# Row copies by SP in place of one gather in 48, in a two-layer graph network

## The chip, the cores and the metric

The kernel runs on one core of a Trainium2 chip. The metric is the device time of one execution in microseconds, the median of a few runs. The engines are named as in the profile: PE (matrix multiplications; PEld loads its weights), DVE (vector engine), ACT (scalar engine), POOL (GpSimd) and SP (SyncE, which here only issues DMAs). Data lies in HBM, in SBUF (128 partitions) and in PSUM, where PE writes its results.

## The reference

Two layers of message passing on 6250 nodes with 128 features and 200,000 edges that are sorted by destination. `_layernorm` and a relu come before each layer, and each layer's output is added to x.

```
# layer 0: attention over a node's incoming edges, 8 heads of 16
z  = (feat @ W).reshape(N, 8, 16);  el, er = <z, attn_l>, <z, attn_r>
e  = leaky_relu(el[src] + er[dst], 0.2)
a  = exp(e - segment_max(e, dst)[dst])
out = segment_sum(z[src] * a, dst) / max(segment_sum(a, dst), 1e-9) + bias

# layer 1: an equivariant message layer
s, v = s @ W_up_s, v @ W_up_v             # per node, before the edges
w0..w3 = silu(silu(edge_feats @ A1 + b1) @ A2 + b2) @ A3      # per edge
mji = [ss*y_s*w0, (vs.y_v)/R3*w3, ss*y_v*w1, vs*y_s*w2]       # ss, vs = s[src], v[src]
out = (segment_sum(mji, dst) / 10) @ W_out
```

What matters here: in both layers every edge needs the row of its source node, `z[src]` with `el[src]` (136 floats) in the first layer and `[s, v][src]` (128 floats) in the second.

## The kernel before

The 200,000 edges are cut into 1563 tiles of 128, one edge to a partition, and the tiles into 98 blocks (NB) of 16 (KB); the last block has 11. A block covers a window of 128 nodes, of which 64 are shared with the next block; a segment sum is a matrix product of a one-hot tile (`one_hot`, L1043) with the tile's messages, summed in one PSUM bank over a block.

**The start** (to about 60 us) normalizes x, multiplies it with W and writes the table `t0` to HBM (`to_table`, L791 to L797, by SP). The source indices of all edges lie in SBUF as `src_col` (partition = edge of the tile, column = tile). A check that the edges are spread evenly is made on the device; its outcome is one word, which every engine loads into a register (`values_load`, L957). After that branch `even_edges` runs.

**Gathers.** `gather` (L832) issues for each tile one indirect DMA on POOL's queue: 128 rows of the table at the indices in one column of `src_col`, into one of the 16 places of a block's buffer `g` (name `z` in the code). There are five such buffers.

**First layer.** One pass of the loop handles three blocks at different stages: `take_rows(g + 3)` issues the gathers three blocks ahead, `logits` (L1112) adds the gathered `el` to `er` for the whole block, `maxima`, `neighbours` and `weights` form the softmax, `weighted` (L1166) scales the rows, `sums` (L1171) does the products. Every second block finishes 128 nodes. `node_x` to `node_s` then normalize them and multiply by W_up, and write a tile of the second table `t1` (`node_s`, L1224 and L1226, by SP, from the tile `sv`, of which there are two). `with_bias` (L1177) loads a tile of x by SP and adds the bias.

**Second layer.** The loop takes units of four tiles, four units to a block. `take_rows(b + 2)` gathers two blocks ahead; `network(b + 1)` computes the edge network one block ahead from two tiles that SP loads (`ft` and `yb`, L1410 and L1412, three buffers each); `messages` (L1458 to L1467, DVE) and `sums1` (L1475) follow. `node1` multiplies finished nodes by W_out, adds x and has SP write the output (L1489, L1491).

**The order of the work.** On PE, DVE and ACT the instructions stand in the order of the program:

```
in_order = {mybir.EngineType.PE, mybir.EngineType.DVE, mybir.EngineType.Activation}
with tc.manual_schedule(engines=in_order), ...
```

On SP and POOL a scheduler orders them. It put all 49 loads of x in one run at the start of the first layer; the writes of `t1` follow as `sv` comes. An engine handles its instructions one after the other, and one that waits for a semaphore holds those behind it. Each DMA of SP counts up one of eight semaphores in turn; a DMA waits, on its semaphore, for the one eight places before it.

Of the kernel before, what the change touches and what calls it, by code (L numbers as in the profile page):

```python
# [9 lines left out]
F32 = mybir.dt.float32  # L10
BF = mybir.dt.bfloat16
I32 = mybir.dt.int32
# [6 lines left out]
P = 128  # L19
# [3 lines left out]
ZW = F + H  # L23
# [940 lines left out]
def even_edges(tc, v):  # L964
# [7 lines left out]
    with ExitStack() as ctx:  # L972
# [3 lines left out]
        def gathered(table, tiles, width):  # L976
            return gather(z_pool.tile([P, KB, ZW], F32, name="g"), table, tiles, width)
# [59 lines left out]

        s_pool = ctx.enter_context(tc.tile_pool(name="fs", bufs=16))

        def one_hot(t, m, iota=iota):  # L1040

            s = s_pool.tile([P, 4, P], F32, name="s")
            nc.vector.tensor_tensor(s[:, :m], iota[:, None, :].to_broadcast([P, m, P]),  # L1043
                                    dloc[:, t : t + m].unsqueeze(2).to_broadcast([P, m, P]),
                                    OP.is_equal)
            return s
# [12 lines left out]
            return carry, agg  # L1059


        in_order = {mybir.EngineType.PE, mybir.EngineType.DVE, mybir.EngineType.Activation}
        with tc.manual_schedule(engines=in_order), \
                tc.tile_pool(name="l0", bufs=2) as l0, \
                tc.tile_pool(name="l0n", bufs=2) as l0n, \
# [106 lines left out]
                                     start=c["o"] + k == 0, stop=c["o"] + k == KT[c["b"]] - 1)  # L1172


            def with_bias(i, n):
                x_i = x_all[:, i : i + n, :]
                nc.sync.dma_start(x_i, xp[i * P : (i + n) * P].rearrange("(j p) f -> p j f", p=P))  # L1177
                nc.vector.tensor_add(x_i, x_i, bias_b[:, None, :].to_broadcast([P, n, F]))

            def node_x(u):  # L1180
# [35 lines left out]
            def node_s(u):  # L1216
                i, n, p_n = u["i"], u["n"], u["p_n"]
                for j in range(n):
                    nc.tensor.matmul(p_n[:, 2 + j, :], u["h_t"][:, j, :], wup, start=True, stop=True)
                sv = l0n.tile([P, 2, P], F32, name="sv")  # L1220
                nc.scalar.activation(sv[:, :n], p_n[:, 2 : 2 + n], AF.Copy, scale=PRE)
                first = i * P - W0
                if i == 0:
                    nc.sync.dma_start(t1[: P - W0, :], sv[W0:, 0, :])  # L1224
                else:
                    nc.sync.dma_start(t1[first : first + n * P].rearrange("(j p) f -> p j f", p=P),  # L1226
                                      sv[:, :n])
# [13 lines left out]
            def take_rows(g):  # L1241
                if 0 < g < NG:
                    c = cs[g]
                    t = c["b"] * KB + c["o"]
                    c["z"] = gathered(t0, range(t, t + c["kt"]), ZW)

            def bank_of(c, bank="p_u"):
                if c["o"] == 0:
# [36 lines left out]
            nc.vector.memset(st["ends"], 0.0)  # L1285
            none = {"kt": 0, "b": 0, "o": 0}
            c5, c4, c3, c2, c1 = cs[NG - 5 :]
            for g in range(NG - 3):
                take_rows(g + 3)
                c, b4 = cs[g], (cs[g - 1] if g else None)  # L1290
                n1 = cs[g + 1] if g + 1 < NG else none
                n2 = cs[g + 2] if g + 2 < NG else none
                nodes = []
                logits(c)
                ends_of(n2, 0)
                if n1 is not none:
                    masks_of(n1)
                turned(n1, 0)
                maxima(c)
                ends_of(n2, 1)  # L1300
# [24 lines left out]
                if b4:  # L1325
                    sums(b4, 0)
                for n in nodes:
                    node_t(n)
                if n1 is not none:
                    er_sum(n1)  # L1330
                ends_of(n2, 3)
                for n in nodes:
                    node_s(n)
                if b4:
                    sums(b4, 8)
                if g == NG - 4:
                    for q in range(4):
                        ends_of(c1, q)
                    masks_of(c1)
                    for q in range(4):  # L1340
                        turned(c1, q)
                        er_of(c1, q)
                    er_sum(c1)
            with_bias(NX - 2, 2)

            logits(c3)
# [43 lines left out]
            node_t(u)  # L1390
            node_x(w)
            node_s(u)
            for step in (node_d, node_h, node_t, node_s):
                step(w)


        with tc.manual_schedule(engines=in_order), \
                tc.tile_pool(name="l1", bufs=3) as l1, \
                tc.tile_pool(name="l1n", bufs=2) as l1n, \
                tc.tile_pool(name="l1_ps", bufs=2, space=PSUM) as l1_ps:  # L1400

            def network(b, step):

                c = blk[b]
                q0, second = step // 2 * 4, step % 2
                if 2 * q0 >= KT[b]:
                    return
                if step == 0:
                    c["ft"] = l1.tile([P, P], F32, name="ft")
                    nc.sync.dma_start(c["ft"], f8[:, b, :])  # L1410
                    c["yb"] = l1.tile([P, KB, 4], F32, name="yb")
                    nc.sync.dma_start(c["yb"], y4[:, b * KB : (b + 1) * KB, :])  # L1412
                    c["h2"] = []
                if step == 3 or 2 * q0 + 8 >= KT[b] and second:
                    c["yp"] = held[:, P + b % 3 * KB * 3 : P + (b % 3 + 1) * KB * 3].rearrange(
                        "p (t i) -> p t i", i=3)
                    nc.scalar.copy(c["yp"], c["yb"][:, :, 1:4])  # L1417
                p_h = l1_ps.tile([P, 4, P], F32, name="p_h")
                if not second:
                    for q in range(4):  # L1420
                        nc.tensor.matmul(p_h[:, q, :], a1p[:, q0 + q, :], c["ft"], start=True, stop=True)  # L1421
                    c["h1"] = l1.tile([P, 4, P], F32, name="h1")
                    nc.scalar.activation(c["h1"], p_h, AF.Silu, bias=b1)  # L1423
                else:
# [53 lines left out]
            def node1(i, agg):  # L1478
                x_i = x_all[:, i, :]
                p_n = l1_ps.tile([P, 4, P], F32, name="p_n", bufs=1)  # L1480
                for q in range(2):
                    nc.tensor.transpose(p_n[:, q, :], agg[:, q * P : (q + 1) * P], ident)
                m_t = l1n.tile([P, 2, P], F32, name="m_t")
                nc.scalar.copy(m_t, p_n[:, :2])
                for q in range(2):
                    nc.tensor.matmul(p_n[:, 2, :], m_t[:, q, :], wout[:, q, :], start=q == 0, stop=q == 1)
                nc.vector.scalar_tensor_tensor(x_i, p_n[:, 2, :], POST, x_i, op0=OP.mult, op1=OP.add)
                if i == 0:
                    nc.sync.dma_start(out[: P - W0, :], x_all[W0:, 0, :])  # L1489
                else:  # L1490
                    nc.sync.dma_start(out[i * P - W0 : (i + 1) * P - W0, :], x_i)  # L1491
# [11 lines left out]

            def take_rows(b):
                if b < NB:
                    blk[b]["z"] = gathered(t1, range(b * KB, b * KB + KT[b]), P)

            for b in range(2):
                take_rows(b)
            for step in range(4):  # L1510
                network(0, step)
# [5 lines left out]
            for i, u in enumerate(us):  # L1517
                b, k0, m = u["b"], u["k0"], u["m"]
                if k0 == 0:
                    take_rows(b + 2)  # L1520
                if b + 1 < NB:
                    network(b + 1, k0 // 4)
                if i + 1 < NU:
# [5 lines left out]
                if ends is not None:  # L1529
# [1 line left out]
                    if ends % 2 == 1:  # L1531
                        done.append((ends // 2, agg))
                    ends = None
                for a in ready:
                    node1(*a)
                ready, done = done, []
                sums1(u)
                if k0 + m == KT[b]:
                    ends = b
            for a in ready:  # L1540
                node1(*a)

            p_u = blk[NB - 1]["p_u"]
            nc.vector.tensor_copy(both[:WB, 0, :], agg[:WB, :])
# [156 lines left out]
```

## Time and profile before

| | us |
|---|---|
| median of 3 runs | 4023.37 (4021.22 to 4023.41) |
| the profiled execution | 4015.26 |
| its span in the profile | 4013.5 |
| first layer, from about 60 to | 2046 |
| second layer, gathers from 2046.9 to | 3997 |
| PE, DVE, ACT, POOL busy | 2837.4, 2191.8, 1374.3, 2993.5 |

| what SP does | count | hold of SP, median ns |
|---|---|---|
| loads of x tiles (L1177) | 49 | 430 |
| writes of `t1` (L1226) | 48 | 320 |
| edge loads (L1410, L1412) | 98 + 98 | 328, 328 |
| outputs (L1491) | 47 | 344 |

A group in the profile names the line, engine and operation, output and input tiles, the count, then busy time in us with the mean of one in ns, then the idle time of the engine ahead of these instructions and what ended most of it. "issue" is idle time in which the engine waited for nothing that the profile shows. Waits name the waiting instruction, what it waited for, the total in us, how often, and the longest. A window's row gives its start and end, its length, busy time with count of PE, PEld, DVE, ACT and POOL, the granted clock of PE, the share of the DMA engines' time in use, and GB/s. Rows of one line give the shortest, median and longest duration of an instruction in ns. SPq, ACTq and so on stand for instructions that the engine's sequencer handles itself: DMA issues, semaphore waits, register loads.

### The profile page before, as it was taken

The page shows a single profiled execution, that of the slowest core. Times are in us where ns is not written, and L with a number is a line of the kernel's source. Part 1 is how long each engine was busy: PE and PEld are TensorE (multiplying, and loading weights), DVE is VectorE, ACT ScalarE, POOL GpSimd, SP SyncE. Part 2 cuts the span into 40 slices and gives each one's busy share as a digit, 9 for nine tenths or more (in the row PEclk, how much of TensorE's full clock was granted, in tenths as well). Part 3 has the DMA queues.
Part 4 walks back from the last instruction along what each step waited for, and adds up shares of the span by engine and source line. Part 5 has one row for each costly group of instructions (what it writes and reads, how often), then busy time and mean ns, then how long its engine had stood idle before and what let it go on. Part 6 is the DMA issues. An engine that isn't in the chain of part 4 may idle for free. (4 is left out here: it accounts for less than half of the span.)

```text
span 4013.5 us, 45637 instructions
## 1 busy us (share of the span) xinstructions
PE 2837.4 (71%) x14592; PEld 2369.6 (59%) x14592; DVE 2191.8 (55%) x5376; ACT 1374.3 (34%) x3450; POOL 2993.5 (75%) x3158
## 2 busy tenths in 40 slices
PE   3666666666666666666677777777787777787787
PEld 3665655565556555555665665565666555666565
DVE  4544444444444444444456666666666666666666
ACT  3322222222222222222333434344434343443443
POOL 6777777777777777777757777777777777777776
PEclk6666666666666666666679999999999999999999
DMA  7222222222222222222212222222222222222221
GB/s 206 57 57 58 57 58 57 58 57 58 57 58 57 58 58 58 57 58 57 58 48 60 60 59 61 59 60 59 60 60 60 59 61 59 60 59 60 60 60 51
DMA packets 174105, 248.25 MB, mean 62 GB/s; under 512 B 70944, under 2 KB 123072, under 8 KB 173856
## 3 DMA queue, kind: packets, MB, share of 16 engines
q0 software_dynamic: 100032, 211.47, 19.7%
q1 hardware_dynamic: 73536, 33.70, 3.1%
q8 instruction: 118, 1.93, 0.2%
q14 instruction: 131, 1.07, 0.1%
q10 hardware_dynamic: 288, 0.07, 0.0%
HBM read 234.73 MB, written 9.99 MB: 61 GB/s over the span
## 5 line engine op out<-in xcount | busy, mean ns | idle before, releaser
L832 POOL DMA_INDIRECT g<-ft,fsrc x3110 | 2959.7, 952 | 975.4 <-issue 892.3
L1475 PE MATMUL p_u<-mj,s 128*128 128x256 f32 x3126 | 802.8, 401 | 354.7 <-DVE mj L1467 354.0
L1475 PEld LDWEIGHTS p_u<-mj,s 128*128 128x128 f32 x3126 | 582.8, 195 | 547.3 <-DVE mj L1467 478.2
L1171 PE MATMUL p_u<-g,s 128*128 128x136 f32 x3062 | 581.8, 369 | 0.5 <-DVE g L1166 0.5
L1171 PEld LDWEIGHTS p_u<-g,s 128*128 128x128 f32 x3062 | 557.2, 273 | 0.6 <-DVE g L1166 0.6
L1458 DVE TENSOR_TENSOR vy<-g,p_i 128x384 f32<-128x384 f32 x391 | 216.5, 554 | 596.3 <-DMA g<-ft,fsrc 569.3
L1442 ACT ACTIVATE p_w<-p_w,yb 128x64 f32<-128x64 f32 x1563 | 450.3, 288 | 113.6 <-PE p_w L1438 73.5
L1112 DVE TENSOR_TENSOR e_s<-g,er 128x128 f32<-128x128 f32 (+1 forms) x98 | 28.4, 290 | 749.3 <-DMA g<-ft,fsrc 749.2
L1438 PE MATMUL p_w<-fa3p,h 128*128 128x256 f32 x1564 | 403.8, 381 | 0.0
L1088 PE MATMUL p_d<-fident,s 128*128 128x128 f32 x1563 | 392.8, 418 | 5.1 <-DVE s L1043 5.1
L1116 PE MATMUL pe<-fident,e_s 128*128 128x128 f32 x98 | 39.7, 406 | 454.0 <-DVE e_s L1113 454.0
L1438 PEld LDWEIGHTS p_w<-fa3p,h 128*128 128x128 f32 x1564 | 285.7, 193 | 120.9 <-issue 57.4
L1081 ACT COPY mk<-p_m 128x385 f32<-128x385 f32 (+1 forms) x99 | 47.6, 481 | 903.1 <-PE p_m L1078 903.1
L1088 PEld LDWEIGHTS p_d<-fident,s 128*128 128x128 f32 x1563 | 318.9, 229 | 43.6 <-DVE s L1043 31.6
L1423 ACT ACTIVATE h<-p_h,fb 128x512 f32<-128x512 f32 x196 | 134.7, 687 | 561.9 <-PE p_h L1421 561.9
L1090 ACT CAST d<-p_d 128x512 bf16<-128x512 f32 x391 | 228.5, 585 | 201.3 <-PE p_d L1088 153.5
L1166 DVE TENSOR_TENSOR g<-g,pe 128x1024 f32<-128x1024 f32 x193 | 225.4, 1208 | 127.8 <-ACT g L1157 125.2
L1116 PEld LDWEIGHTS pe<-fident,e_s 128*128 128x128 f32 x98 | 16.6, 169 | 470.6 <-issue 462.6
L1043 DVE TENSOR_TENSOR s<-p_i,fdloc 128x512 f32<-128x512 f32 x391 | 266.2, 681 | 14.5 <-ACT p_i L1417 14.5
L1043 DVE TENSOR_TENSOR s<-fiota,fdloc 128x512 f32<-128x512 f32 x391 | 265.6, 681 | 5.9 <-ACT fmasks L1036 5.8
L1428 ACT ACTIVATE h<-p_h,fb 128x512 f32<-128x512 f32 x196 | 134.7, 687 | 362.0 <-PE p_h L1425 362.0
L1462 DVE TENSOR_REDUCE vd<-vy 128x128 f32<-128x384 f32 x391 | 228.9, 585 | 0.0
(172 smaller groups left out, 3417.5 us busy)
## 6 DMA issues: line engine op xcount, KB each, us to landing
g<-ft,fsrc POOLq DMA_INDIRECT x3110, 2.5
ft<-in_e_f_dram SPq DMA_DIRECT2D x98, 64.0 KB
yb<-in_e_y_dram SPq DMA_DIRECT2D x98, 32.0 KB
fx_all<-in_e_xp_dram SPq DMA_DIRECT2D x48, 64.0 KB
ft<-sv SPq DMA_DIRECT2D x47, 64.0 KB
out_dram<-fx_all SPq DMA_DIRECT2D x47, 64.0 KB
ft<-zt SPq DMA_DIRECT2D x6, 408.0 KB
fxs<-in_e_xp_dram SPq DMA_DIRECT2D x6, 384.0 KB
```

The costliest lines, as they stand in the source:

```text
L832: nc.gpsimd.indirect_dma_start(out=to[:, k, :width], out_offset=None, in_=table, in_offset=bass.IndirectOffsetOnAxis(ap=src_col[:, t : t + ...
L1043: nc.vector.tensor_tensor(s[:, :m], iota[:, None, :].to_broadcast([P, m, P]), dloc[:, t : t + m].unsqueeze(2).to_broadcast([P, m, P]), OP. ...
L1088: nc.tensor.transpose(p_d[:, k, :], c["s"][q][:, k, :], ident)
L1090: nc.scalar.copy(d[:, :m], p_d[:, :m])
L1166: nc.vector.tensor_mul(zh, zh, p_a[:, k0 : k0 + m].unsqueeze(3).to_broadcast([P, m, H, D]))
L1171: nc.tensor.matmul(c["p_u"][:, :ZW], c["s"][k // 4][:, k % 4, :], c["z"][:, k, :], start=c["o"] + k == 0, stop=c["o"] + k == KT[c["b"]] - 1)
L1423: nc.scalar.activation(c["h1"], p_h, AF.Silu, bias=b1)
L1438: nc.tensor.matmul(w[:, k : k + n].rearrange("p k a u -> p (k a u)"), c["h2"][q // 4][:, q % 4, :], a3p[:, :n].rearrange("p k f -> p (k f) ...
L1442: nc.scalar.activation(w[:, k, ::2, :], w[:, k, ::2, :], AF.Copy, scale=c["yb"][:, k0 + k, 0:1])
L1458: nc.vector.tensor_mul(vy, v_n, y_p)
L1462: nc.vector.tensor_reduce(vd, vy.rearrange("p t i u -> p t u i"), AX.X, OP.add)
L1475: nc.tensor.matmul(blk[b]["p_u"][:, :MW], u["s"][:, k, :], u["mj"][:, k, :], start=k0 + k == 0, stop=k0 + k == KT[b] - 1)
```

## The change

In blocks 3, 6, ... 93 (31 in each layer) POOL gathers 15 tiles, not 16. The 128 rows of the 16th are copied by SP, one DMA for each row, from an address in a register of SP. The byte offsets of these rows are prepared at the start of `even_edges`: the columns of `src_col` for all blocks' last tiles are converted to floats, turned by PE so that a block's 128 indices lie in one partition, and multiplied by the row's size in bytes (`at`, one tile for each layer). SP loads 32 offsets at a time from there, four times for a block. The rows go to a tile of their own (`r`, three buffers); `filled` has ACT copy it into the 16th place of the block's buffer.

`rows_by_row` is a generator that stops after every four rows; `rows_until` advances it up to a quota that grows with the block that the loop is at and that runs three blocks ahead of it.

SP joins the engines in the order of the program, and so its other DMAs are placed by hand: a tile of x is loaded in every second pass (`node_rows`), the writes of `t1` come one pass later (`node_out`), the edge loads two blocks ahead (`edge_rows`, four buffers each), the outputs in the second unit of a block (`node_out1`).

```diff
+        by_row = [b for b in range(3, NB - 2) if b % 3 == 0]
+        row_pool = ctx.enter_context(tc.tile_pool(name="frow", bufs=3))
+        at = [const.tile([P, P], I32, name=f"fat{i}") for i in range(2)]
+        with tc.tile_pool(name="fat_ps", bufs=1, space=PSUM) as at_ps:
+            col = const.tile([P, P], F32, name="fcol")
+            n = NB - 1
+            nc.vector.tensor_copy(col[:, :n], v["src_col"][:, KB - 1 : n * KB : KB])
+            p_c = at_ps.tile([P, P], F32, name="p_c")
+            nc.tensor.transpose(p_c[:n], col[:, :n], ident)
+            for i, w in enumerate((ZW, P)):
+                nc.vector.tensor_scalar(at[i][:n], p_c[:n], float(4 * w), None, op0=OP.mult)
+
+        def rows_by_row(layer, table, width):
+            flat = table.rearrange("r f -> (r f)").bitcast(mybir.dt.uint8)
+            size = 4 * width
+            for b in by_row:
+                to = row_pool.tile([P, width], F32, name="r")
+                rows_by_row.tiles[layer, b] = to
+                for e in range(P):
+                    if e % 32 == 0:
+                        _, offs = nc.values_load_multi_w_load_instructions(
+                            at[layer][b : b + 1, e : e + 32], engines=[mybir.EngineType.SP],
+                            min_val=0, max_val=(NX * P - W0 - 1) * size,
+                            skip_runtime_bounds_check_because="a row of the table")
+                    nc.sync.dma_start(to[e : e + 1, :].bitcast(mybir.dt.uint8),
+                                      flat[ds(offs[e % 32], size)].unsqueeze(0))
+                    if e % 4 == 3:
+                        yield
+
+        def rows_until(rows, block):
+            while rows_until.n < (block + 3) * P / 12 and next(rows, 0) is None:
+                rows_until.n += 1
+
+        def filled(layer, b, z, width):
+            if b in by_row:
+                nc.scalar.copy(z[:, KB - 1, :width], rows_by_row.tiles.pop((layer, b)))
...
-        in_order = {mybir.EngineType.PE, mybir.EngineType.DVE, mybir.EngineType.Activation}
+        in_order = {mybir.EngineType.PE, mybir.EngineType.DVE, mybir.EngineType.Activation,
+                    mybir.EngineType.SP}
...
-                    c["z"] = gathered(t0, range(t, t + c["kt"]), ZW)
+                    c["z"] = gathered(t0, range(t, t + c["kt"] - (c["b"] in by_row)), ZW)
...
             for g in range(NG - 3):
                 take_rows(g + 3)
+                filled(0, g, cs[g]["z"], ZW)
+                rows_until(rows, g + 0.5)
+                for n in late:
+                    node_out(n)
+                if g % 2 == 0 and g // 2 + 2 < NX - 2:
+                    node_rows(g // 2 + 2, 1)
+                rows_until(rows, g + 1)
...
-                    blk[b]["z"] = gathered(t1, range(b * KB, b * KB + KT[b]), P)
+                    blk[b]["z"] = gathered(t1, range(b * KB, b * KB + KT[b] - (b in by_row)), P)
...
                 if k0 == 0:
                     take_rows(b + 2)
+                    filled(1, b, blk[b]["z"], P)
+                    edge_rows(b + 2)
+                if k0 == 4:
+                    while late:
+                        node_out1(late.pop())
+                rows_until(rows, b + (k0 + 4) / KB)
```

More of the change, by code (lines that the diff above doesn't have):

```diff
@@ L1038, in even_edges @@
         s_pool = ctx.enter_context(tc.tile_pool(name="fs", bufs=16))
+        by_row = [b for b in range(3, NB - 2) if b % 3 == 0]
[25 more added lines that the diff above has]
+                        yield
+        rows_by_row.tiles = {}
+        def rows_until(rows, block):
[4 more added lines that the diff above has]
+                nc.scalar.copy(z[:, KB - 1, :width], rows_by_row.tiles.pop((layer, b)))
         def one_hot(t, m, iota=iota):
@@ L1172, in sums, with node_rows @@
                                      start=c["o"] + k == 0, stop=c["o"] + k == KT[c["b"]] - 1)
+            def node_rows(i, n):
+                nc.sync.dma_start(x_all[:, i : i + n, :],
+                                  xp[i * P : (i + n) * P].rearrange("(j p) f -> p j f", p=P))
             def with_bias(i, n):
                 x_i = x_all[:, i : i + n, :]
[L1177 removed]
                 nc.vector.tensor_add(x_i, x_i, bias_b[:, None, :].to_broadcast([P, n, F]))
@@ L1219, in node_s, with node_out @@
                     nc.tensor.matmul(p_n[:, 2 + j, :], u["h_t"][:, j, :], wup, start=True, stop=True)
-                sv = l0n.tile([P, 2, P], F32, name="sv")
+                sv = u["sv"] = l0n.tile([P, 2, P], F32, name="sv")
                 nc.scalar.activation(sv[:, :n], p_n[:, 2 : 2 + n], AF.Copy, scale=PRE)
+            def node_out(u):
+                i, n, sv = u["i"], u["n"], u["sv"]
                 first = i * P - W0
@@ L1287, in even_edges @@
             c5, c4, c3, c2, c1 = cs[NG - 5 :]
+            rows, rows_until.n, late = rows_by_row(0, t0, ZW), 0, []
+            for i in range(2):
+                node_rows(i, 1)
             for g in range(NG - 3):
                 take_rows(g + 3)
+                filled(0, g, cs[g]["z"], ZW)
[5 more added lines that the diff above has]
+                rows_until(rows, g + 1)
                 c, b4 = cs[g], (cs[g - 1] if g else None)
@@ L1333, in even_edges @@
                     node_s(n)
+                late = nodes
                 if b4:
@@ L1343, in even_edges @@
                     er_sum(c1)
+            node_rows(NX - 2, 2)
+            for n in late:
+                node_out(n)
             with_bias(NX - 2, 2)
@@ L1392, in even_edges @@
             node_s(u)
-            for step in (node_d, node_h, node_t, node_s):
+            node_out(u)
+            for step in (node_d, node_h, node_t, node_s, node_out):
                 step(w)
@@ L1400, in even_edges, with edge_rows @@
                 tc.tile_pool(name="l1_ps", bufs=2, space=PSUM) as l1_ps:
+            def edge_rows(b):
+                if b < NB:
+                    c = blk[b]
+                    c["ft"] = l1.tile([P, P], F32, name="ft", bufs=4)
+                    nc.sync.dma_start(c["ft"], f8[:, b, :])
+                    c["yb"] = l1.tile([P, KB, 4], F32, name="yb", bufs=4)
+                    nc.sync.dma_start(c["yb"], y4[:, b * KB : (b + 1) * KB, :])
             def network(b, step):
@@ L1408, in network @@
                 if step == 0:
[L1409 to L1412, printed above, removed]
                     c["h2"] = []
@@ L1487, in node1, with node_out1 @@
                 nc.vector.scalar_tensor_tensor(x_i, p_n[:, 2, :], POST, x_i, op0=OP.mult, op1=OP.add)
+                return i
+            def node_out1(i):
+                x_i = x_all[:, i, :]
                 if i == 0:
@@ L1505, in take_rows @@
                 if b < NB:
-                    blk[b]["z"] = gathered(t1, range(b * KB, b * KB + KT[b]), P)
+                    blk[b]["z"] = gathered(t1, range(b * KB, b * KB + KT[b] - (b in by_row)), P)
+            rows, rows_until.n, late = rows_by_row(1, t1, P), 0, []
             for b in range(2):
+                edge_rows(b)
                 take_rows(b)
@@ L1533, in even_edges @@
                     ends = None
-                for a in ready:
-                    node1(*a)
+                late += [node1(*a) for a in ready]
                 ready, done = done, []
@@ L1539, in even_edges @@
                     ends = b
-            for a in ready:
-                node1(*a)
+            for i in late + [node1(*a) for a in ready]:
+                node_out1(i)
             p_u = blk[NB - 1]["p_u"]
```

## The prediction

> **What bounds the kernel now.** I read the busy table with the waits of the gather engine first, then the windows of the two layers, then the timeline of SP.
>
> ```profile
> PE 2837.4 (71%) x14592; PEld 2369.6 (59%) x14592; DVE 2191.8 (55%) x5376; ACT 1374.3 (34%) x3450; POOL 2993.5 (75%) x3158
> ...
> L832 POOL DMA_INDIRECT g<-ft,fsrc x3110 | 2959.7, 952 | 975.4 <-issue 892.3
> ```
>
> No engine is near 100%. POOL's 75% misleads: of its 975.4 us of idle time before gathers, 892.3 are "issue", waiting for nothing that the profile shows. The other engines wait for its gathers:
>
> ```profile
> POOL g L832 <- issue: 892.3, 2928, 0.3
> DVE e_s L1112 <- DMA g<-ft,fsrc: 749.2, 95, 9.1
> DVE vy L1458 <- DMA g<-ft,fsrc: 569.3, 347, 3.5
> POOL g L832 <- DMA ft<-sv: 27.9, 1, 27.9
> ```
>
> A gather is 952 ns busy and 0.3 us of issue, 1.25 us in all, back to back. The windows say the same of each layer (POOL is the fifth busy time, with its count behind it):
>
> ```profile
> 170.00:2000.00 1830.00, 1188.36 (x6943) 1090.18 (x6943) 794.69 (x1774) 521.57 (x1093) 1388.39 (x1450) 0.65 0.22 58
> 2100.00:3950.00 1850.00, 1445.27 (x6577) 1111.59 (x6578) 1223.37 (x3103) 743.90 (x2085) 1398.34 (x1483) 0.98 0.21 60
> ```
>
> 1850/1483 = 1.248 us and 1830/1450 = 1.262 us for one gather. A block has 16 of them: about 20 us, three blocks 60 us. POOL sets the pace from 60 us to 2018 us and from 2047 us to 3997 us. DVE waits 749.2/98 = 7.6 us in each block of the first layer and 569.3/98 = 5.8 us in each block of the second, so another engine becomes the bound only once far more than one gather of 16 is gone.
>
> **What the change takes away.** Blocks 3, 6, ... 93 of each layer: 31 x 2 = 62 gathers of 3110. 62 x 1.248 = 77.4 us, all on POOL's path. With the rows there in time the kernel would take 4023.4 - 77.4 = 3946 us. Three blocks then take 47 x 1.25 = 58.7 us.
>
> **What it adds on SP.** In place of one gather stand 128 copies of one row and 4 register loads of 32 addresses each, in SP's own order, 62 times: 7936 copies and 248 loads. SP has now 386 copies in all and mostly waits for others, so it has room; the question is whether one tile's rows fit into 58.7 us. Three sums are needed.
>
> ```profile
> L1410 SPq DMA_DIRECT2D ft<-in_e_f_dram x98: 327/328/432, 2046.2 to 3921.6; - x98
> ...
> L1177 SPq DMA_DIRECT2D fx_all<-in_e_xp_dram x49: 328/430/807, 66.7 to 90.7; - x49
> ...
> L957 SPq TENSOR_LOAD <-fok x1: 474/474/474, 43.6 to 43.6; - x1
> ```
>
> The copies. No one-row copy is in the trace, nor one with its address in a register. A 128-row copy holds SP for 328 ns when nothing is before it (minimum, median and maximum stand in the row), and in a burst 430 ns. Starts are some 44 ns further apart than that (2046.16 + 0.33 to 2046.54 in the timeline). So a pitch of 0.372 us, or 0.474 in a burst. I take 0.372: [...]a table write of 6 x 128 rows (L797, 359 ns) holds SP hardly longer than one of 128, so the hold is not made of rows. [...] Between 0.33 (no gap, a shorter hold) and 0.474: 128 copies take 42 to 61 us, taken 128 x 0.372 = 47.6 us. The eight completion semaphores let eight copies fly at once; the f8 copies land 1.9 us after their issue, 0.24 us for each of eight, below the pitch, so that wait is covered.
>
> The loads. The row: one register in 474 ns. If 32 come at that price, 4 loads are 1.9 us. [...] here they come from SBUF, and no run here shows more than one register. [...] The two prices lie far apart: 1.9 or 26.7 us for a tile. I take 26.7, as an estimate. The trace leans that way: the same load takes 474 ns on SP and 473 on ACT for a single word, some ten times a MOVE (about 40) or a compare-and-branch on SP (49), so most of it is a trip to memory; 32 words are 32 trips unless the sequencer overlaps them, and nothing in the trace shows it do so.
>
> The rest of SP's order for three blocks. First layer: 1.5 loads of x and 1.5 table writes, 3 x 0.372 = 1.1 us. Second layer: 6 edge loads and 1.5 outputs, 7.5 x 0.372 = 2.8 us. They were there before; now they share SP with the rows.
>
> Sum for three blocks: 47.6 + 26.7 + 1.1 = 75.4 us in the first layer, 47.6 + 26.7 + 2.8 = 77.1 in the second, against 58.7 that POOL then needs. **SP becomes the bound**, and the gathers taken off POOL are worth nothing.
>
> **What is late then.** ACT copies the rows into the block's last place (`filled`) ahead of everything else of that block; in its queue behind it stand the masks, the casts of the turned one-hot tiles and the exponent, and PE and DVE wait for those. In the second layer also the edge loads come late, since SP issues those of block b + 2 behind the rows of an earlier quota. Waits at the row buffers (three) and at `sv` (two) only move the lag, since SP's whole order is the sum above.
>
> First layer: SP begins the rows at about 70 us of the span (the copy before them, L1023, ends at 66.7), 31 x 75.4 = 2337 us, then blocks 93 to 97. Before, their logits begin at 1946 and the last table write is at 2044: 98 us at POOL's pace; with their gathers already waiting in five buffers I take 75. End at 70 + 2337 + 75 = 2482. Second layer: 31 x 77.1 = 2390 us; the quota runs three blocks ahead, so some seven blocks follow, at PE's 1445.27/1850 = 78% of 20 us, 15.6 us each, and 17 us of end (3997 to 4013.5): 126. Span 2482 + 2390 + 126 = 4998. The profiled execution took 4015.3 us for its span of 4013.5, and the median of the runs is 4023.4, 9.9 above the span. **About 5008 us.**
>
> Costed at nothing: 62 copies by ACT (L1157, 128 x 128 in 0.27 us, 17 us in all), hidden in ACT's 903.1 us of waiting at the masks and 561.9 at the networks; three operations by DVE and one by PE at the start, hidden behind the first gathers, which already run. If that cover were gone they would cost some 20 us. 7936 packets more on DMA engines with a share of 0.22: nothing. The x loads leave the start; POOL issues gathers there without a gap (63 in the 80 us from 90 to 170), so nothing is gained.
>
> **Rivals.**
> *Rows in time, faster.* Loads of 32 at the price of one: 47.6 + 1.9 + 1.1 = 50.6 us, 8 us inside 58.7; 3946 us. For it: 128 copies alone fit by the 328 ns row. [...] It decides at (58.7 - 47.6 - 1.1)/4 = 2.5 us a load, 65 ns for each further register; equal to before (60 us) at 2.8 us.
> *Loads cheap, copies at the burst's pitch.* 128 x 0.474 = 60.7, with 1.9 and 3 x 0.474 = 1.4: 64.0 us, in the second layer 60.7 + 1.9 + 7.5 x 0.474 = 66.2. Then 70 + 31 x 64.0 + 75 + 31 x 66.2 + 126 = 4307, 4317 us. For it: 47 of the 49 copies in that burst come slower than 328. It decides from 0.434 us a copy.
> *The removed gather was covered anyway,* no change: against it stand the 892.3 us of issue; it would need POOL to wait for a buffer, and the waits show none beyond 28 us.
>
> **How the numbers follow.** SP bound by its loads 0.61; SP bound by copies or by loads of middling price 0.11 (between 4050 and 4450); rows in time 0.27; within 0.2% (8 us, about what a measurement of this kernel can tell from no change) 0.01 by itself, and 0.01 of the middle case lies there. So faster 0.27, same 0.02, slower 0.71. The likeliest has its own range: 130 ns a register gives loads of 4.5 us, 66.7 and 68.4 us for three blocks and 4468 us; 240 ns a register with 0.40 us a copy gives 7.9 us, 84 and 86 us, and some 5550. I give it 4450 to 5400. With faster at 0.27 the range has to reach down to it: 3938 to 5400.
>
> **What would show it.** In the profile after: POOL's count of gathers 62 lower, and its idle time put down to buffers, no longer to issue; the load of 32 registers at about 6.7 us in SP's rows (wrong if under 2.5); the row copies near 330 ns with a pitch of 0.37; ACT waiting long at `filled` for row copies; SP without long waits; each layer longer in the windows. It is wrong if the load turns out short: then POOL's issue stays the largest idle time and the time is near 3946.

## The result and the profile after

The changed kernel takes **3958.97 us** (median of 4 runs, 3956.9 to 3960.89). The kernel before, run beside it, took 4022.3 us (4 runs, 4019.46 to 4023.41). The ratio is **0.984**, with a 95% interval of 0.9826 to 0.9861: 63 us faster, where the prediction said 985 us slower. It went the way of the rival that had the rows in time (3946 us), 13 us short of it.

The profiled run of after took 3960.89 us with a span of 3959.1 us. That of before had a span of 4013.5 us, so the two profiles differ by 54.4 us. Single runs of the kernel before scatter by some 5 us to each side on different chips; steps are taken apart below on the two profiles.

In some of the runs further down the kernel before itself took 5177 to 5295 us, for a cause that stays open (in the trace of after_psum 1056 of SP's 7936 MOVEs took 0.6 to 0.9 us, in after none); each such run is given with the kernel before that ran beside it, and no size is taken from it.

The page of the kernel after, its busy times and the row of the gathers:

```profile
PE 2823.8 (71%) x14593; PEld 2368.9 (60%) x14593; DVE 2189.6 (55%) x5379; ACT 1390.4 (35%) x3512; POOL 2955.5 (75%) x3096
...
L832 POOL DMA_INDIRECT g<-ft,fsrc x3048 | 2921.8, 959 | 957.7 <-issue 873.5
```

The 62 gathers are gone (3110 to 3048), yet POOL's gather time fell by only 2959.7 - 2921.8 = 37.9 us, where 62 x 0.944 would be 58.5: the mean gather has become 959 ns, from 952. POOL still waits for nothing but its own issue (873.5 of 957.7 us). The waits of the kernel after (who waited, for what: us in total, times, longest):

```profile
POOL g L832 <- issue: 873.5, 2864, 0.3
DVE e_s L1156 <- DMA g<-ft,fsrc: 697.0, 90, 10.7
...
DVE vy L1527 <- DMA g<-ft,fsrc: 374.6, 227, 3.7
...
POOL g L832 <- DMA ft<-sv: 28.3, 1, 28.3
```

The buffers never hold POOL up, and DVE still waits for gathers, less in total than before (697.0 for 749.2, and 374.6 for 569.3). So POOL is the bound after as before. The windows of the two layers of after (length; then PE, PEld, DVE, ACT and POOL busy, each with its count; TensorE clock, DMA share, GB/s):

```profile
170.00:2000.00 1830.00, 1191.38 (x7008) 1091.50 (x7009) 801.99 (x1794) 534.98 (x1135) 1392.72 (x1434) 0.65 0.27 60
2100.00:3950.00 1850.00, 1487.23 (x6778) 1154.74 (x6778) 1258.03 (x3199) 773.54 (x2177) 1392.61 (x1476) 0.97 0.24 61
```

They hold the puzzle of this case. In the first layer POOL's busy time in the same 1830 us went up, 1388.39 to 1392.72, with 16 instructions fewer. The second layer shows nothing of this: its mean gather is 943.6 ns in both kernels. (Its gathers now end before 3950, so its count here isn't a pitch.)

What SP does now, by its two new lines in the kernel after (duration in ns: least, median, most; first and last start):

```profile
L1063 SPq TENSOR_LOAD <-fat x248: 1904/2171/2455, 68.8 to 3771.0; - x124
```

```profile
L1067 SPq MOVE r<-ft x7936: 29/29/38, 76.9 to 3783.4; - x199
L1067 SPq DMA_DIRECT2D r<-ft x7936: 227/228/418, 82.2 to 3783.5; - x199
...
  ACT g L1081: 11.6, 15
```

A load of 32 registers takes 2.17 us, not the estimated 6.7. A one-row copy holds SP for 228 ns, with a MOVE of 29 ns ahead of it; the median distance from copy to copy is 0.323 us. ACT waited for the rows 11.6 us in 62 copies. SP now waits for the others, as the first lines of SP's own waits in after show:

```profile
SPq L1276 <- ACT sv L1268: 252.8, 23, 40.6
SPq L1564 <- DVE fx_all L1556: 123.8, 20, 39.5
```

### The profile page after: what moved, and what is told of

It reads as the page before. It is cut to its first block, busy times and chain, and to the rows that moved or that the text cites. A ratio compares the mean times of both kernels' runs of the same rounds, so it can differ in the third digit from the quotient of the medians.

```text
span 3959.1 us, 62173 instructions
## 1 busy us (share of the span) xinstructions
PE 2823.8 (71%) x14593; PEld 2368.9 (60%) x14593; DVE 2189.6 (55%) x5379; ACT 1390.4 (35%) x3512; POOL 2955.5 (75%) x3096
## 3 DMA queue, kind: packets, MB, share of 16 engines
q1 hardware_dynamic: 89408, 37.92, 3.7%
## 5 line engine op out<-in xcount | busy, mean ns | idle before, releaser
L832 POOL DMA_INDIRECT g<-ft,fsrc x3048 | 2921.8, 959 | 957.7 <-issue 873.5
L1544 PE MATMUL p_u<-mj,s 128*128 128x256 f32 x3126 | 794.3, 398 | 263.7 <-DVE mj L1536 261.9
L1527 DVE TENSOR_TENSOR vy<-g,p_i 128x384 f32<-128x384 f32 x391 | 215.6, 551 | 462.4 <-DMA g<-ft,fsrc 374.6
L1156 DVE TENSOR_TENSOR e_s<-g,er 128x128 f32<-128x128 f32 (+1 forms) x98 | 28.4, 290 | 735.0 <-DMA g<-ft,fsrc 697.0
L1492 ACT ACTIVATE h<-p_h,fb 128x512 f32<-128x512 f32 x196 | 134.7, 687 | 568.8 <-PE p_h L1490 567.5
L1086 DVE TENSOR_TENSOR s<-p_i,fdloc 128x512 f32<-128x512 f32 x391 | 266.0, 680 | 14.5 <-ACT p_i L1486 14.5
L1086 DVE TENSOR_TENSOR s<-fiota,fdloc 128x512 f32<-128x512 f32 x391 | 265.8, 681 | 5.9 <-ACT fmasks L1036 5.8
L1490 PE MATMUL p_h<-ft,fa1p 128*128 128x128 f32 x1568 | 217.7, 284 | 62.5 <-DMA ft<-in_e_f_dram 62.4
L1490 PEld LDWEIGHTS p_h<-ft,fa1p 128*128 128x128 f32 x1568 | 214.2, 200 | 79.3 <-issue 63.7
```

The source lines that it names most:

```text
L832: nc.gpsimd.indirect_dma_start(out=to[:, k, :width], out_offset=None, in_=table, in_offset=bass.IndirectOffsetOnAxis(ap=src_col[:, t : t + ...
L1527: nc.vector.tensor_mul(vy, v_n, y_p)
L1544: nc.tensor.matmul(blk[b]["p_u"][:, :MW], u["s"][:, k, :], u["mj"][:, k, :], start=k0 + k == 0, stop=k0 + k == KT[b] - 1)
```

## The experiments

Each of load4_b, copies_only_e, no_copies_e and after_psum_d is one execution, with one of the kernel before beside it.

**Loads of 4 registers in place of 32 (load4_b).** The rows are the same, with eight times as many loads. If the prediction's mechanism is sound and only its price of a load was wrong, a dear enough load must bring the forecast slowdown about.

```diff
-                    if e % 32 == 0:
+                    if e % 4 == 0:
...
-                            at[layer][b : b + 1, e : e + 32], engines=[mybir.EngineType.SP],
+                            at[layer][b : b + 1, e : e + 4], engines=[mybir.EngineType.SP],
...
-                                      flat[ds(offs[e % 32], size)].unsqueeze(0))
+                                      flat[ds(offs[e % 4], size)].unsqueeze(0))
```

> The same kernel as load4 (register loads of 4 offsets in place of 32), run again because in the first round the kernel before itself took 5190 us and not 4022, so that its numbers can't be set beside this study's. Where the kernel before takes its 4022: SP's order bounds it, 64.4 us for three blocks in the first layer and 65.7 in the second, about 4310 us with a load of 4 at about 640 ns; near 3959 to 4020 if SP's occupancy is hidden.

Measured: 4378.67 us, with the kernel before at 4024.72. The load's row in this kernel:

```profile
L1063 SPq TENSOR_LOAD <-fat x1984: 324/564/831, 67.4 to 4259.0; - x199
```

And its waits:

```profile
POOL g L832 <- issue: 942.4, 2865, 9.1
DVE e_s L1156 <- ACT g L1081: 783.5, 31, 28.3
...
ACT g L1081 <- DMA r<-ft: 573.7, 48, 25.8
```

This is what the prediction foresaw for the change itself: ACT waits for rows (573.7 us, 11.6 in after), and DVE waits for ACT behind it (783.5 us at `e_s`). From its first row copy of a layer to its last, SP needs 2096.98 - 80.37 = 2016.6 us in the first layer and 4260.67 - 2182.10 = 2078.6 in the second: 65.1 and 67.0 us for a tile's rows and what goes with them. In these two stretches SP waited for others for only 0.7 and 4.7 us, so they are its own work. (This run's own forecast, about 4310, was 69 us low: it had 64.4 and 65.7 us for a tile.) Put into the prediction's sum, 70 + 31 x 65.1 + 75 + 31 x 67.0 + 126 = 4366 us; the span is 4376.9. So the way from SP's sum to the time holds to 11 us. Only the durations in it were wrong.

The row also prices the load. One register took 474 ns before (a single load), four take 564, 32 take 2171 (medians): (2171 - 474)/31 = 55 ns for each further register, on the average, and 30 ns for the first three.

**SP's new order alone (sp_order).** No block has its rows copied; the x loads, edge loads and table writes stay where the change put them.

```diff
-        by_row = [b for b in range(3, NB - 2) if b % 3 == 0]
+        by_row = []
```

> No block is copied by rows (the list of such blocks is empty), all else of the change stays: SP in program order, x loads and writes placed by hand. If the whole gain comes from the 62 gathers, this is the kernel before: 4022 us, within 8. If the new order of SP has a part in it, it lies below, at most near 3959.

Measured: 5270.0 us with the kernel before at 5276.85, ratio 0.999 (0.9973 to 1.0013). Beside such a kernel before, it says no more than that the order alone moved nothing there. copies_only_e, next, holds the same order beside a kernel before of 4015.45 us, and takes the same time.

**The row copies alone (copies_only_e).** All 16 gathers are kept, the 128 copies and four loads are made too, and the copied tile is thrown away.

```diff
-                    c["z"] = gathered(t0, range(t, t + c["kt"] - (c["b"] in by_row)), ZW)
+                    c["z"] = gathered(t0, range(t, t + c["kt"]), ZW)
...
-                    blk[b]["z"] = gathered(t1, range(b * KB, b * KB + KT[b] - (b in by_row)), P)
+                    blk[b]["z"] = gathered(t1, range(b * KB, b * KB + KT[b]), P)
...
-                nc.scalar.copy(z[:, KB - 1, :width], rows_by_row.tiles.pop((layer, b)))
+                rows_by_row.tiles.pop((layer, b))
```

> The same kernel as copies_only, again because the kernel before took 5248 us beside the last one. All 7936 row copies, unread, beside all of POOL's gathers: if the copies bring the longer overlap of gathers and one-hots, about 4042 with first-layer gathers near 974 ns; if not, 4022.

Measured: 4015.53 us, the kernel before 4015.45. The gathers of this kernel's page:

```profile
L832 POOL DMA_INDIRECT g<-ft,fsrc x3110 | 2961.3, 952 | 975.5 <-issue 892.9
```

7936 copies and 248 loads cost nothing, and the gathers are as long as before (952 ns). My first idea of the missing gain, that the copies' packets get in the gathers' way, falls with this run.

**15 gathers without the copies (no_copies_e).** The other half: the gather is taken out and no rows are fetched in its stead; ACT fills the 16th place from a constant tile.

```diff
+        fixed = const.tile([P, ZW], F32, name="ffixed")
+        nc.vector.memset(fixed, 0.5)
...
-                to = row_pool.tile([P, width], F32, name="r")
-                rows_by_row.tiles[layer, b] = to
-                for e in range(P):
+                rows_by_row.tiles[layer, b] = fixed[:, :width]
+                for e in range(0):
...
-                nc.scalar.copy(z[:, KB - 1, :width], rows_by_row.tiles.pop((layer, b)))
+                nc.scalar.copy(z[:, KB - 1, :width], fixed[:, :width])
```

> The row copies and their register loads are left out; 15 gathers in every third block as in the changed kernel, and the 16th place is filled from a constant, so the row's values are not the table's. Theory A: the order of 15 gathers, by moving where the first one-hot of a block falls in the cadence of the gathers, lengthens the first layer's gathers by itself: about 3959 us, first-layer gather mean 973 ns, last row of a block landing 2.56 us after its gather's start. Theory B: the lengthening needs the copies and the 15-gather order together: about 3945 us, gather mean 960 ns, landing 2.49 us.

Measured: 3959.85 us, the kernel before 4019.61. Its gathers:

```profile
L832 POOL DMA_INDIRECT g<-ft,fsrc x3048 | 2923.2, 959 | 956.5 <-issue 868.3
```

That is the time of the changed kernel, with its long gathers, without one row copy. So the two halves add up: the copies are hidden, the missing gain belongs to taking the gather out, and the rival's 3946 was too low for a reason that has nothing to do with SP.

**The first layer's one-hot comparison with one input from PSUM (after_psum_d).** The long gathers lie where DVE compares a block's destinations with a row of numbers (`one_hot`, L1086), in the first layer with both inputs in SBUF. The timeline of DVE in one block of after (start us, duration us):

```profile
1029.03 0.29 DVE L1156 TENSOR_TENSOR e_s<-g,er 128x128 f32<-128x128 f32 x1 [6.46 <-DMA g<-ft,fsrc]
...
1029.56 0.68 DVE L1086 TENSOR_TENSOR s<-fiota,fdloc 128x512 f32<-128x512 f32 x1
...
1031.07 0.67 DVE L1086 TENSOR_TENSOR s<-fiota,fdloc 128x512 f32<-128x512 f32 x1
```

And POOL's at the same place:

```profile
1030.12 0.95 POOL L832 DMA_INDIRECT g<-ft,fsrc  x1 [0.30 <-issue]
1031.37 1.18 POOL L832 DMA_INDIRECT g<-ft,fsrc  x1 [0.30 <-issue]
1032.86 0.94 POOL L832 DMA_INDIRECT g<-ft,fsrc  x1 [0.30 <-issue]
```

The first comparison ends at 1030.24, 0.12 us after a gather's start: the gather takes 0.95. The second ends at 1031.74, 0.37 us after one: the gather takes 1.18. The second layer compares with one input from PSUM (`s<-p_i,fdloc`), and there the mean gather is 943.6 ns in both kernels. If the comparison's two inputs in SBUF are what lengthens a gather, a first layer with one input from PSUM lets the gathers alone too. The edit puts the row of numbers into the unused quarter of the bank that `p_er` lies in:

```diff
+            held0 = l0_ps.tile([P, 512], F32, name="p_er")
+            nc.scalar.copy(held0[:, :P], iota)
...
-                    c["s"].append(one_hot(c["b"] * KB + c["o"] + 4 * q, min(4, c["kt"] - 4 * q)))
+                    c["s"].append(one_hot(c["b"] * KB + c["o"] + 4 * q, min(4, c["kt"] - 4 * q),
+                                          held0[:, :P]))
...
-                    if q == 0:
-                        c["p_er"] = l0_ps.tile([P, KB, 3, H], F32, name="p_er")
+                    c["p_er"] = held0[:, P:].rearrange("p (t s h) -> p t s h", s=3, h=H)
```

> The same kernel as after_psum (the changed kernel, first layer's one-hots from a copy of iota in PSUM), one look, because where the earlier rounds ran the kernel before took 5190 to 5280 us. If the longer gathers come from the one-hots that they overlap: first-layer gathers at 944 ns, about 3914 us. If from the row copies' DMA traffic: 3935 to 3959.

Measured: **3917.15 us**, the kernel before 4018.47, faster than both kernels of this case. Its gathers, by its page:

```profile
L832 POOL DMA_INDIRECT g<-ft,fsrc x3048 | 2881.0, 945 | 957.6 <-issue 865.9
```

I sorted the first layer's gathers (170 to 1900 us) of five profiles by whether a comparison was still running 150 ns or more after the gather's start. "Excess" is the sum of (duration - 944 ns); the last column is how long after the start of a block's last gather `e_s` begins (median).

```
kernel                     gathers  covered >=150 ns  their excess  others' excess  e_s begins
before                       1370        109             19.2 us        0.0 us       2608 ns
copies alone                 1370        111             19.3 us        0.1 us       2614 ns
15 gathers, no copies        1353        179             39.4 us        0.0 us       2836 ns
after                        1355        181             38.0 us        0.0 us       2835 ns
after, input from PSUM       1384        224             -0.1 us        1.5 us       2827 ns
```

The whole excess lies in the covered gathers, and there are more of them with 15 gathers. With one input from PSUM even more gathers are covered, 224, and none takes more than 957 ns. That settles the cause: the comparison with both inputs in SBUF, not the time at which it runs.

The last column says why more are covered. The first comparison starts 0.53 us after `e_s` and takes 0.68; the third gather after the block's last starts 3 x 1.248 = 3.744 us after it. Before, the comparison ends at 2.608 + 0.53 + 0.68 = 3.818, only 0.07 us into that gather; after, at 4.045, 0.30 us into it. (The second comparison, 1.5 us behind the first, reaches far into the fourth gather in both kernels.)

Why `e_s` comes 0.23 us later stands in the traces too. The gathers count up eight semaphores in turn. Ahead of `e_s` DVE waits for all eight, mostly two to a wait instruction, in an order that the program fixes. With 16 gathers in every block, twice the turn, a block's last gather always has a semaphore of the last of these waits. Each block of 15 shifts the turn by one. Then the last gather's semaphore often stands in an earlier wait, in blocks of 16 gathers as well, and DVE still has to go through the waits behind it, about 0.1 us each, though what they wait for has landed before. For blocks 8 to 92 of the first layer (medians for `e_s`, means for the third gather):

```
waits behind the last     blocks   e_s begins after     third gather's
gather's own                       the last landing     excess over 944 ns
before, none                85          123 ns                  6 ns
after, none                 15          121                    31
after, one                  20          178                   107
after, two                  22          276                   206
after, three                24          393                   287
after, four                  4          484                   403
```

So the third gather's excess grows with the number of these waits. In the median `e_s` begins 0.275 us after the last landing, 0.123 before: 0.15 of the 0.23 us. The other 0.08 is the landing itself, 2560 ns after the gather's start and 2484 before; why it is later is not settled.

**Runs whose times settle nothing.** In these the kernel before beside them took 5190 to 5277 us. Two of the edits have not been shown yet. Every second block by rows asks where SP's room ends:

```diff
-        by_row = [b for b in range(3, NB - 2) if b % 3 == 0]
+        by_row = [b for b in range(4, NB - 2) if b % 2 == 0]
...
-            while rows_until.n < (block + 3) * P / 12 and next(rows, 0) is None:
+            while rows_until.n < (block + 1) * P / 8 and next(rows, 0) is None:
```

> The changed kernel with the row copies in every second block (46 blocks in each layer, from 4 to 94), their quota set to run three blocks ahead of the loop as before. POOL then needs 31 x 1.25 = 38.7 us for two blocks, SP 41.3 + 8.9 + 0.8 = 51.0 in the first layer and 52.3 in the second. If SP's own order is the bound: 70 + 46 x 51.0 + 75 + 46 x 52.3 + 126 = 5023, about 5030 us. If POOL stayed the bound: about 3905 us.

> The same kernel as every2 (rows in every second block, 46 in each layer), on a chip where the kernel before takes its 4022. If SP's own order is the bound: 41.3 + 8.9 + 0.8 = 51.0 us for two blocks in the first layer and 52.3 in the second against POOL's 38.7, about 5030 us. If POOL stayed the bound: about 3905 us.

The input from PSUM in the kernel before, without the change (the edit of after_psum_d), asks whether the two gains are independent:

> The kernel before, with the first layer's one-hots read from a copy of iota in PSUM. Its first-layer gathers have 24.5 us over 944 ns each; if the overlap with DVE's one-hots is the cause, that goes: about 3998 us. Else 4022.

> The same kernel as before_psum. If the overlap with DVE's one-hots makes the kernel before lose 24.5 us in its first-layer gathers: about 3998 us. Else 4022.

The others repeat edits shown above. The expectations of copies alone:

> SP copies all 7936 rows into their own tiles, but POOL still gathers all 16 tiles of every block and nothing reads the copies. Theory A (the copies disturb the first layer's gathers, directly or by moving the one-hots of DVE against them): about 20 us over the kernel before, 4042, with first-layer gathers at about 974 ns mean and second-layer gathers still at 944. Theory B (the copies are free, the lost part of the gain has another cause): 4022.

> The same kernel as copies_only, on a chip where the kernel before takes its 4022 us. Theory A (the copies disturb the first layer's gathers, directly or by moving the one-hots of DVE against them): about 20 us over the kernel before, 4042. Theory B (the copies are free): 4022.

> The same kernel as copies_only (all 7936 row copies, unread, beside all of POOL's gathers). With the one-hots shown to be what lengthens gathers: if the copies bring the longer overlap (they land gathers later and so shift the one-hots), about 4042 with first-layer gathers near 974 ns; if the overlap grew because 15 gathers stand in place of 16, 4022.

Of 15 gathers without copies (the sixteenth place filled from a constant):

> POOL gathers 15 tiles in the 62 blocks, SP copies no rows; ACT fills the 16th place from a constant tile (the rows of these tiles are left out). Theory A: the full 77 us, 3945. Theory B (what is lost comes from gathering 15 in place of 16 itself): 3959, as with the copies.

> The same kernel as no_copies (the rows of the 62 tiles are left out, their place is filled from a constant). Theory A: the full 77 us, 3945. Theory B: 3959, as with the copies.

Of loads of 4 registers:

> The changed kernel with register loads of 4 offsets in place of 32, 32 loads a tile. By a line through the two prices seen (474 ns for one register, 2171 for 32: 55 ns for each further one) a load of 4 takes about 640 ns, 22 us a tile with its gap. With copies at a pitch of 0.323 us a tile is 41.3 + 22 + 1.1 = 64.4 us in the first layer and 65.7 in the second, over the 58.7 that POOL needs: SP is the bound, 70 + 31 x 64.4 + 75 + 31 x 65.7 + 126 = 4304, about 4310 us. If SP's occupancy is not what decides (other work still hides it), it stays near 3959 to 4020.

Of the changed kernel with the input from PSUM:

> The changed kernel with the first layer's one-hots read from a copy of iota in PSUM (in the unused quarter of the bank of p_er), so that DVE's comparison no longer has both inputs in SBUF. If the longer gathers come from the one-hots that they overlap, gathers fall to 944 ns in the first layer too and the 45 us above that go: about 3914 us. If they come from the row copies' DMA traffic alone, the 20 us that the change added stay: about 3935 to 3959.

> The same kernel as after_psum. If the longer gathers come from the one-hots that they overlap: gathers at 944 ns in the first layer, about 3914 us. If from the DMA traffic of the row copies: 3935 to 3959.

> The same kernel as after_psum (the changed kernel, first layer's one-hots from a copy of iota in PSUM), alone, because in the two earlier rounds the kernel before took 5260 to 5280 us. If the longer gathers come from the one-hots that they overlap: first-layer gathers at 944 ns, about 3914 us. If from the row copies' DMA traffic: 3935 to 3959.

Median us of each, with the kernel before beside it, and the ratio of the two:

```
kernel                          this      before   ratio
copies alone (copies_only)     6247.83   5276.85   1.184
copies alone (copies_only_b)   6231.39   5259.20   1.185
copies alone (copies_only_d)   6214.09   5247.61   1.184
no copies (no_copies)          5229.43   5276.85   0.991
no copies (no_copies_b)        5195.55   5259.20   0.988
loads of 4 (load4)             6366.08   5190.22   1.227
every second block (every2)    7138.08   5190.22   1.375
every second block (every2_d)  7250.69   5239.65   1.384
after, PSUM (after_psum)       6309.58   5276.85   1.196
after, PSUM (after_psum_b)     6266.50   5259.20   1.192
after, PSUM (after_psum_c)     6168.58   5190.51   1.188
before, PSUM (before_psum)     5318.53   5190.22   1.025
before, PSUM (before_psum_b)   5416.18   5259.20   1.030
```

Here every kernel with row copies took 18% or more longer than the kernel before, and the ones without them stayed within 3% of it. Four of these edits have a run beside a kernel before of about 4020 us, told above, and that one counts. Of every second block, and of the PSUM input without the row copies, there is none: where SP's limit lies and what the kernel before would gain from the PSUM input stays open. Their traces do show the gathers' lengths. In before_psum 89 first-layer gathers were covered for 150 ns or more, and their excess is -0.1 us in all (81 and 0.1 us in before_psum_b); in sp_order, with both inputs in SBUF, it is 49 us for 140. So the PSUM input takes the excess away without row copies too.

## Why the prediction was wrong

**The step that failed is the price of the register load: "I take 26.7, as an estimate".** Two prices were set against each other for a tile's four loads, 1.9 us (32 registers at the price of one) and 26.7 us (an estimate of mine, 6.7 us a load, that no trace or run had shown). Measured are 4 x 2.17 = 8.7 us. I had named the break-even myself, 2.5 us a load or 65 ns for each further register; the measured 55 lies just below it. The estimate is three times too much (26.7 us for 8.7). The argument that leaned to it ("32 words are 32 trips unless the sequencer overlaps them") is refuted by the four-register load: 564 ns, where four trips at 474 would be 1896. What the 474 ns of one word are made of, no trace shows.

**The copies' pitch was too high as well**, 0.372 us taken from 128-row copies, bounds 0.33 to 0.474; measured 0.323, just outside. The hold of a one-row copy is 228 ns where the 128-row ones show 328. "The hold is not made of rows" was drawn from 128 against 6 x 128 rows and does not carry to one row. That alone would hardly have turned the result: with the measured load and the pitch as taken, the first layer has 47.6 + 8.7 + 1.1 = 57.4 us, inside 58.7, and the second 59.1, over it by 0.4. With both as measured (medians) the sums are 41.3 + 8.7 + 1.1 = 51.1 and 52.8 us for three blocks, 87% and 90% of what POOL needs. The rival's own sum, 50.6 us, meets this by luck: its load was far too cheap (1.9 us a tile for 8.7) and its copies too dear (47.6 for 41.3). The burst pitch of 0.474, the rival at 4317, doesn't occur.

**POOL as the bound was right**, and so was a gather's worth. The second layer, from its first gather to its last, went from 3996.8 - 2046.9 = 1949.9 us to 3941.6 - 2029.9 = 1911.7: 38.2 us, by 31 x 1.248 = 38.7. The first layer gave only 17.9 (1975.7 to 1957.8). Its mean gather went from 960.1 to 973.8 ns, and the excess over 944 ns, over the whole layer, from 25.2 to 45.7 us; 38.7 - 20.5 = 18.2. The two layers give 56.1 us, the gap between them and the ends take back 1.7, which makes the 54.4 us of the two spans. So **the rival's term "62 x 1.248" was right in size and left out what a changed rhythm does to the other gathers.** The row that could have warned of it was in the profile before: 1.262 us for a first-layer gather, against 1.248 in the second, read off the windows and not asked about.

**The smaller steps.** ACT's 62 copies cost 302 ns each, 18.7 us (17 foreseen), hidden. DMA's share went from 0.22 to 0.27 in the first layer, harmless; the hardware queue moved 89408 - 73536 = 15872 packets more, two for a row (the row and one of 4 bytes), not the one that I counted. The semaphore of a one-row copy is updated twice, 0.40 and 1.42 us after its start (medians), where that of a 128-row copy is updated mostly 16 times; what this costs SP is inside the 0.323 us. The x loads' leaving the start gained nothing, as said: the first gather into `g` starts at 63.4 us, 62.9 before. That SP would be without long waits was wrong with the bound: it waits 252.8 us for `sv`. Of the signs named, POOL's idle time at issue and a load under 2.5 us were those of the rival, and both came.

## What to carry to other kernels

Where a forecast turns on one price between two far ends, look at the break-even first: here it was 65 ns for each further register (2.5 us a load), the measured price 55 (2.17 us), and neither end (0.474 or 6.7 us a load) was near it. An estimate that no trace shows doesn't decide between them. A queue that mostly waits can take thousands of small transfers, at 0.32 us each here, off an engine that is the bound, as long as the sum stays below the bound's pace (51 us of 59 here). And when work is taken off the bounding engine, look at what lengthens the rest of its work: mean durations that differ between two stages for the same instruction (960 and 944 ns) are a gain to be had, and here it was worth another 42 us. Count the waits as well: taking one gather of 16 out moved the last one's semaphore forward in the order of DVE's waits, and that lengthened other gathers.

## What the runs showed of the hardware

- A sequencer's load of registers from SBUF took 474 ns for one (474 to 479 on SP in five traces), 564 for four, 2171 for 32 (medians).
- A one-row copy with its address in a register held SP for 228 ns; a MOVE of 29 ns stands ahead of it, and the pitch was 0.323 us. A 128-row copy with a fixed address held it for 328 at the least in the x loads before.
- A gather that started under a DVE comparison with both inputs in SBUF became longer by what was left of the comparison less 127 ns (median of 652 gathers with 150 ns or more left, in four traces; 0.37 us left, 0.24 longer); with less left it was not longer (excess of 0.0 or 0.1 us in all). A comparison that started after the gather did not lengthen it (median 0 in 838). With one input in PSUM there was no effect in 224 cases.
- A wait instruction of DVE whose semaphores had already been counted up still held `e_s` back by about 0.1 us ((484 - 121)/4 = 91 ns on the average, medians of after).
